# Attention weights transposed before they are scaled, with the scale applied to the values on leaving PSUM

## The chip, the core and the metric

The kernel runs on one core of one Trainium2 chip. The metric is the device time of one execution in microseconds (us). Three timed runs of the kernel before gave 3035.5, 3037.48 and 3040.55 us. The core has a matrix engine (TensorE, PE in the profile; its weight loads are PEld), VectorE (DVE), ScalarE (ACT) and GpSimd (POOL), and SyncE (SP), which here only issues DMAs. Each engine works through its own instructions in order.

## The reference

The input x has shape (4, 1024, 512). A graph attention layer comes first (part L0), then a transformer block conditioned on a vector (part L1). The change is within the attention of L1:

```python
qkv = x @ W_qkv                      # 16 heads of 64
attn = jnp.einsum('bqhd,bkhd->bhqk', q, k) * scale
attn = jax.nn.softmax(attn, axis=-1)
out = jnp.einsum('bhqk,bkhd->bqhd', attn, v).reshape(Bq, Tq, INNER)
return out @ W_out + b_out
```

Each of the 4 batch elements has 1024 rows, so each head has a 1024 x 1024 matrix of weights. Everything is in float32.

## The kernel before

The work has three stages: the graph attention (to about 400 us), the attention of L1 (to about 2235 us) and the MLP (to the end). Many of the large products are built of seven half-size products instead of eight, with sums made ahead by GpSimd and afterwards by VectorE.

**Slots.** The attention runs over 4 batch elements, 8 pairs of heads and 8 tiles of 128 query rows, that is 256 slots (variable `s`; `NS` = 256). A slot handles one tile `t` of one pair of heads; the two heads are `j` = 0 and 1. Two slots make a block `k` of 256 query rows (`QT` = 2 tiles). Within a slot:

- `scores` (L1151): eight matmuls, 64 rows deep, the two heads side by side, fill two PSUM tiles `psc` of 128 x 1024, one for each head. There are two such tiles in all, so the next slot's scores need this slot's exponentials done.
- `largest` (L1165): VectorE takes the negated row maximum of each head (`mx`, L1167).
- `weights` (L1170): ScalarE computes the exponential into an SBUF tile `w` (four buffers) and sums it along the row into `sm` (L1173).
- `scaled` (L1176): VectorE inverts the sum (L1178); head 0's weights are multiplied by it on ScalarE (L1180), head 1's on GpSimd (L1182).
- `turn` (L1184): VectorE transposes 32 x 32 pieces of `w` into the tile `wd` (L1191). `wd` holds one head's weights for both tiles of a block; its tag has three buffers, taken in turn. After the second tile, SP issues four DMAs of 256 KB (L1195) which move the four groups of 32 partitions of `wd` to their places in `wT`, so that keys lie along partitions. `wT` holds both heads of a block and has two buffers.
- `attend` (L1055): four slots after the block's first slot, 32 matmuls of values by weights, two heads side by side, sum up 128 x 256 in the PSUM tile `pav`; ScalarE copies it into `oT` (L1076).
- `out_step` (L1124): a part of the output projection, in the PSUM tile `pu`; VectorE adds it to the rows `xr` (L1148).

**Order.** The main loop (L1497) writes the order of a slot by hand. It first transposes head 0 of the slot before (`turn(..., 0)`), then does what is kept in `later` (copies and sums which empty PSUM after a projection step, on ScalarE and VectorE), then the scores, the two maxima, `early` (a part of the output projection that falls into the slot), the two exponentials, head 0's scaling, the transposition of head 1 of the slot before, and head 1's scaling. Last comes `emit`: the work that a planner (L1367 to L1447) has put into this slot, which is loads, attend, steps of the projections to q, k and v, parts of the output projection, and sums on GpSimd. The planner balances TensorE's work over the slots by the units given with each piece. Every engine gets its instructions in this order.

```python
            if before is not None:
                turn(*before[0], 0)
            while later:
                later.pop(0)()
```

The four lines above open a slot (L1498). VectorE's order in a slot is thus: transposition of head 0 (slot before), sums of `later`, maximum of head 0, maximum of head 1, an addition of `early`, inverse of sum 0, transposition of head 1 (slot before), inverse of sum 1, and the sums that `emit` brings.

Of the kernel before, what the change touches and what calls it, by code (L numbers as in the profile page):

```python
# [12 lines left out]
F32 = mybir.dt.float32  # L13
I32 = mybir.dt.int32
AF = mybir.ActivationFunctionType
ALU = mybir.AluOpType
# [3 lines left out]
P = 128  # L20
S = 1024
F = 512
FC = F // P
NT = S // P
# [8 lines left out]
H, D = 16, 64  # L33
# [8 lines left out]
def cond_block_kernel(  # L42
# [27 lines left out]
    nc = tc.nc  # L70
# [4 lines left out]
    def row(ap):  # L75

        return ap.unsqueeze(0)
# [46 lines left out]

    x1d = [tc.dram_tile([P, F], F32, name=f"x1d{i}") for i in range(NTA)]
    gated = tc.dram_tile([P, F], F32, name="gated")
    qrd = tc.dram_tile([B, F], F32, name="qrd")
    vrd = [tc.dram_tile([KV, F], F32, name=f"vrd{d}") for d in range(2)]
    x2d = [tc.dram_tile([P, F], F32, name=f"x2d{i}") for i in range(NTA)]
# [2 lines left out]
    with ExitStack() as gctx:  # L132
        KC0 = GH * 2 * NG // P
        HF = GH * NG
        gp = gctx.enter_context(tc.tile_pool(name="gp", bufs=1))
# [49 lines left out]
        with ExitStack() as sctx:  # L185
# [13 lines left out]
            rows = sp.tile([N_VEC, P], F32, name="rows")  # L199
# [8 lines left out]
            ws, gboB = [], sp.tile([KV, 2, F], F32, name="gboB")  # L208
# [365 lines left out]
        later = []  # L574
# [366 lines left out]
    with ExitStack() as actx:  # L941
        ap_ = actx.enter_context(tc.tile_pool(name="ap", bufs=1, reuse_waits="tile"))
        q1, q2 = (ps.tile([P, F], F32, name=n, tag=n) for n in ("q1", "q2"))
        two_banks = {"ma": q2, "mb": q1, "mc": q1, "md": q2}
        NP = 2 * NGRP
# [3 lines left out]
        QB = 256  # L949
        QT = QB // P  # L950
        NB = S // QB
        wout, gate = {}, {}
        vt, oT, xr, wn, wd, wT = {}, {}, {}, {}, {}, {}

        turns = []

# [98 lines left out]
        def attend(b, gp, k, a=0, z=KC):  # L1055

            if a == 0:
                pav[0] = ps.tile([P, F], F32, name="pav", tag="pav")[:, :QB]
            po = pav[0]
            g, p = divmod(gp, 2)  # L1060
            w = wT[b, gp, k]
            for m in range(a, z):
                for j in range(2):
                    nc.tensor.matmul(  # L1064
                        po[j * D : (j + 1) * D, :],
                        lhsT=vt[b, g][:, m, p * P + j * D : p * P + (j + 1) * D],
                        rhs=w[:, j, :, m, :],
                        start=(m == 0),
                        stop=(m == KC - 1),
                    )  # L1070
            if z < KC:
                return
            u, i = divmod(k, 2)
            if i == 0:
                oT[b, gp, u] = op_.tile([P, F], F32, name="oT", tag="oT", bufs=6)
            nc.scalar.copy(  # L1076
                oT[b, gp, u][:, i * QB : (i + 1) * QB].rearrange("p (t u q) -> p u t q", t=QT, u=4),
                po.rearrange("p (u t q) -> p u t q", t=QT, u=4),
            )

        def project(b, g, n):
# [69 lines left out]
        def scores(b, gp, t):  # L1151
            sc = [ps.tile([P, S], F32, name="psc", tag="sc", bufs=2) for _ in range(2)]
            for n in range(2):
                for j in range(2):
                    q = slice(j * D, (j + 1) * D)
                    nc.tensor.matmul(  # L1156
                        sc[j][:, n * F : (n + 1) * F],
                        lhsT=qT[b, gp][q, t * P : (t + 1) * P],
                        rhs=kT[b, gp][q, n * F : (n + 1) * F],
                        start=True,  # L1160
                        stop=True,
                    )
            return sc

        def largest(sc):  # L1165
            mx = ap_.tile([P, 1], F32, name="mx", tag="mx", bufs=4)
            nc.vector.tensor_reduce(mx, sc, axis=AX.X, op=ALU.max, negate=True)  # L1167
            return mx

        def weights(sc, mx):  # L1170
            w = ap_.tile([P, S], F32, name="w", tag="w", bufs=4)
            sm = ap_.tile([P, 1], F32, name="sm", tag="sm", bufs=4)
            nc.scalar.activation(w, sc, AF.Exp, bias=mx, accum_out=sm)  # L1173
            return w, sm

        def scaled(j, w, sm):  # L1176

            nc.vector.reciprocal(sm, sm)  # L1178
            if j == 0:
                nc.scalar.mul(w, w, sm)  # L1180
            else:
                nc.gpsimd.tensor_scalar(w, w, sm, None, ALU.mult)  # L1182

        def turn(b, gp, t, j):  # L1184

            k, at = divmod(t, QT)
            if at == 0:
                wd[j] = ap_.tile([P, 4 * KC, QT, U], F32, name="wd", tag="wd", bufs=3)
                if j == 0:
                    wT[b, gp, k] = ap_.tile([P, 2, 4, KC, QT * U], F32, name="wT", tag="wT", bufs=2)  # L1190
            nc.vector.transpose(wd[j][:, :, at, :], wn.pop((b, gp, t, j)).rearrange("p (m k) -> p m k", k=U))  # L1191
            if at == QT - 1:
                flat = wd[j].rearrange("p m t q -> p (m t q)")
                for u in range(4):
                    nc.sync.dma_start(  # L1195
                        wT[b, gp, k][:, j, u].rearrange("p m q -> p (m q)"), flat[U * u : U * (u + 1), :]
                    )
# [11 lines left out]
        def halves():  # L1209

            two = [ps.tile([P, S], F32, name="up", tag="sc", bufs=2) for _ in range(2)]
            return {n: two[k // 2][:, k % 2 * F : (k % 2 + 1) * F] for k, n in enumerate(("ma", "mb", "mc", "md"))}
# [5 lines left out]
        NS = B * NP * NT  # L1218
# [21 lines left out]
        for b in range(B):  # L1240
# [22 lines left out]
            for gp in range(NP):  # L1263
                g, p = divmod(gp, 2)
                at = s0 + gp * NT
# [12 lines left out]
                for k in range(NB):  # L1278
                    lo = at + QT * k + LAG
                    if gp == NP - 2:  # L1280

                        for h in range(2):
                            add(lo + h, lo + h, 1, 1, attend, b, gp, k, h * KC // 2, (h + 1) * KC // 2)
                        continue
                    add(lo, lo + (lo < NS - 8), 2, 1, attend, b, gp, k)
# [60 lines left out]
        for i in range(4):  # L1346
            at = NS - (10, 9, 6, 3)[i]
# [109 lines left out]
        def fill_of(s):  # L1457
            return [k for k in range(len(fill)) if where[k] == s]

        def emit(a, b):  # L1460


            for s in range(a, b):
                steps = {where[k] for k in chain}
                second = [k for k in outs if where[k] == s][1:]

                def place(k):
                    if k in inside:
                        at = 2.5 if s - 1 in steps else 0.5
                        if k in chain:  # L1470
                            return at
                        if k in second:
                            return 3.5
                        return min(at, 2) + 0.1 if s in steps else 2
                    return fill[k][3]

                for k in sorted(fill_of(s), key=lambda k: (place(k), k)):
                    if k not in done_early:
                        fill[k][4]()
                if s in steps and s - 1 not in steps and sum(fill[k][2] for k in fill_of(s)) >= 3:  # L1480
                    while later:
                        later.pop(0)()
# [3 lines left out]
        def early(s):  # L1486

            two = [k for k in outs if where[k] == s]
            sums = [k for k in fill_of(s) if fill[k][3] == -1]
            for k in two[: len(two) - 1] + sums:  # L1490
                fill[k][4]()
                done_early.add(k)

        row_sum(0, 2)
        emit(-3, 0)
        before = None
        for s in range(NS + 1):  # L1497
            if before is not None:  # L1498
                turn(*before[0], 0)
            while later:  # L1500
                later.pop(0)()
            if s < NS:
                b, r = divmod(s, NP * NT)
                gp, t = divmod(r, NT)
                sc = scores(b, gp, t)
                mx = [largest(sc[j]) for j in range(2)]
                early(s)
                ws = [weights(sc[j], mx[j]) for j in range(2)]
                now = ((b, gp, t), ws)
                scaled(0, *ws[0])  # L1510
            if before is not None:
                turn(*before[0], 1)
            before = None
            if s < NS:
                scaled(1, *ws[1])
                for j in range(2):
                    wn[(*now[0], j)] = ws[j][0]
                before = now
            if s < NS:
                emit(s, s + 1)  # L1520
        sc_banks = halves()
        late = []
        second = with_four(
# [25 lines left out]
    with ExitStack() as mctx:  # L1549
# [53 lines left out]
        for k in range(NB2):  # L1603
            b = k * VB // NT
# [3 lines left out]
            for p in range(2 if k == 0 else 0, 4):  # L1608
# [12 lines left out]
                elif p == 3:  # L1621
                    sums = []
                    for j in range(2):
                        o = [w2x[j][:, n] for n in range(3)]
                        q, r = w2s[j], w2s[2 + j]
# [97 lines left out]
```

## Time and profile before

| what | value |
|---|---|
| timed runs | 3035.5, 3037.48, 3040.55 us |
| profiled execution, its span | 3034.2 us |
| instructions | 41780 |
| DVE transposition of 128x1024 (L1191) | 512 x 1235 ns |
| DVE maximum of 128x1024 (L1167) | 512 x 1211 ns |
| ACT exponential (L1173) | 512 x 1115 ns |
| ACT scaling (L1180) | 256 x 1137 ns |
| POOL scaling (L1182) | 256 x 2846 ns |
| ACT copy of the values (L1076) | 128 x 359 ns (median) |
| DVE addition to the rows (L1148), 128x512 from PSUM | 210 x 683 ns |
| DMAs wT<-wd | 1024 of 256 KB |
| queue q1 (SP's DMAs) | 282256 packets, 415.03 MB, 53.8% of 16 engines' span |

The profile is of one execution; its span, from the first instruction to the last, is 3034.2 us, and the only other times at hand are the three timed runs, which lie 1.3 to 6.4 us above it. "Busy" is the time in which an engine works on data; issuing DMAs and waiting aren't busy. A row of the timeline gives start, length, engine, line and operation, what it writes and reads, and how often; brackets at its end give the idle time of the engine before it and who ended it. A row with x2 or x8 stands for so many instructions in a row. The chain of waits is followed back from the last instruction, at each step to what released it; "SPq" is the issuing of a DMA, "DMA" the time from its issue to its landing.

### The profile page before, as it was taken

The numbers are of one execution on the slowest core, as the hardware profiler recorded it, in microseconds if no ns is written. First come the engines' busy times: TensorE is split into PE (matmuls) and PEld (weight loads), VectorE is DVE, ScalarE is ACT, GpSimd is POOL, SyncE is SP. The second block draws the span as 40 slices with busy tenths as digits, with TensorE's granted clock in tenths as the row PEclk, the third lists the DMA queues.
The fourth block names the chain that finished last, engine by engine and source line by source line (L and its number), as shares of the span: only waits on it lengthen the run. The fifth ranks groups of instructions, "written<-read, shape, count | busy, mean of one in ns | idle before, by whom it ended". The sixth has DMA issues, their size and how long they took to land.

```text
span 3034.2 us, 41780 instructions
## 1 busy us (share of the span) xinstructions
PE 2999.3 (99%) x15317; PEld 1980.2 (65%) x15317; DVE 1999.6 (66%) x2836; ACT 1432.0 (47%) x2368; POOL 1339.4 (44%) x922
## 2 busy tenths in 40 slices
PE   9999999999999999999999999999999999999999
PEld 6666655555555555555555555555568888888888
DVE  3888867777878877878787878877863222222322
ACT  3344456555755565755555755556641221112211
POOL 1444456555656655656655656655721110111010
PEclk9999999999999999999999999999999999999999
DMA  6433357777868777768777868766871010101110
GB/s 201 140 118 121 117 129 180 162 171 179 192 157 210 181 168 179 192 155 211 187 159 180 191 159 205 189 162 164 203 196 63 14 49 28 49 21 35 35 42 15
DMA packets 282695, 417.90 MB, mean 138 GB/s; under 512 B 28968, under 2 KB 101092, under 8 KB 282492
## 3 DMA queue, kind: packets, MB, share of 16 engines
q1 hardware_dynamic: 282256, 415.03, 53.8%
q8 instruction: 123, 2.02, 0.3%
q14 instruction: 80, 0.66, 0.1%
q10 hardware_dynamic: 236, 0.20, 0.0%
HBM read 120.93 MB, written 25.76 MB: 48 GB/s over the span
## 4 chain that ended last, share of the span: by engine, by line
PE 83%; DVE 7%; ACT 3%; POOL 3%; issue 2%; DMA 2%; SPq 1%; POOLq 0%; DVEq 0%; ACTq 0%
PE q L533 19%; PE psc L1156 15%; PE pav L1064 13%; PE pu L1139 6%; PE mbd L533 5%; PE mbu L533 5%; PE mad L533 4%; PE mau L533 3%; PE mcd L533 2%; PE mdd L533 2%; PE mdu L533 2%; PE mcu L533 2%; DVE mx L1167 1%; ACT w L1173 1%; POOL t L742 1%
## 5 line engine op out<-in xcount | busy, mean ns | idle before, releaser
L1182 POOL TENSOR_SCALAR w<-w,sm 128x1024 f32<-128x1024 f32 x256 | 728.6, 2846 | 701.5 <-DVE sm L1178 686.4
L1173 ACT ACTIVATE w<-psc,mx 128x1024 f32<-128x1024 f32 x512 | 570.7, 1115 | 642.6 <-DVE mx L1167 641.6
L1191 DVE STREAM_TRANSPOSE wd<-w 128x1024 f32<-128x1024 f32 x512 | 632.2, 1235 | 109.3 <-ACT w L1180 96.0
L1167 DVE TENSOR_REDUCE mx<-psc 128x1 f32<-128x1024 f32 x512 | 599.2, 1211 | 80.2 <-PE psc L1156 77.0
L1156 PE MATMUL psc<-kT,qT 64*128 64x512 f32 x2048 | 526.9, 615 | 3.1 <-ACT kT L1024 1.4
L1064 PE MATMUL pav<-wT,v 128*64 128x256 f32 x4096 | 482.1, 383 | 1.2 <-DMA wT<-wd 0.6
L1064 PEld LDWEIGHTS pav<-wT,v 128*64 128x64 f32 x4096 | 296.1, 137 | 224.0 <-issue 86.0
L1156 PEld LDWEIGHTS psc<-kT,qT 64*128 64x128 f32 x2048 | 201.6, 186 | 220.5 <-issue 151.2
L1180 ACT ACTIVATE w<-w,sm 128x1024 f32<-128x1024 f32 x256 | 291.0, 1137 | 0.0
L512 POOL TENSOR_TENSOR tx<-hT 128x512 f32<-128x512 f32 x8 | 10.3, 1288 | 596.5 <-ACT hT L448 596.5
L1148 DVE TENSOR_TENSOR xr<-pu,xr 128x512 f32<-128x512 f32 x210 | 143.5, 683 | 78.9 <-PE pu L1139 78.7
L533 PE MATMUL q<-hT,wqk 128*128 128x512 f32 (+1 forms) x396 | 181.2, 581 | 1.0 <-DVE q L547 1.0
L555 ACT COPY mbu<-mau 128x512 f32<-128x512 f32 x30 | 17.1, 570 | 276.5 <-PE mau L533 276.5
L719 PE MATMUL pa<-kp,sfT 128*128 128x320 f32 x512 | 143.5, 433 | 1.4 <-ACT sfT L694 1.4
L533 PEld LDWEIGHTS q<-hT,wqk 128*128 128x128 f32 x396 | 74.7, 190 | 80.9 <-issue 78.2
L533 PE MATMUL q<-tx,ex 128*128 128x512 f32 (+1 forms) x264 | 123.5, 591 | 1.8 <-POOL tx L618 1.3
L719 PEld LDWEIGHTS pa<-kp,sfT 128*128 128x128 f32 x512 | 94.8, 190 | 38.2 <-ACT sfT L694 1.9
L679 PE MATMUL pf<-wx,xT 128*128 128x512 f32 x256 | 116.0, 596 | 0.0
L533 PE MATMUL mad<-w,hs 128*128 128x256 f32 x512 | 113.1, 379 | 0.0
L533 PEld LDWEIGHTS mad<-w,hs 128*128 128x128 f32 x512 | 97.3, 190 | 13.2
L1139 PE MATMUL pu<-wout,oT 128*128 128x256 f32 x360 | 98.4, 396 | 4.2 <-DVE xr L1148 3.7
L1139 PEld LDWEIGHTS pu<-wout,oT 128*128 128x128 f32 x360 | 62.6, 189 | 59.3 <-issue 31.6
(309 smaller groups left out, 4590.7 us busy)
## 6 DMA issues: line engine op xcount, KB each, us to landing
wT<-wd SPq DMA_DIRECT2D x1024, 256.0 KB
wqk<-in_w_qkv SPq DMA_DIRECT2D x64, 256.0 KB
xT<-in_xt SPq DMA_DIRECT2D x32, 256.0 KB
xs<-in_x SPq DMA_DIRECT2D x32, 256.0 KB
x1d<-xs SPq DMA_DIRECT2D x32, 256.0 KB
xl<-x1d SPq DMA_DIRECT2D x32, 256.0 KB
wv<-in_w_qkv SPq DMA_DIRECT2D x32, 256.0 KB
xr<-x1d SPq DMA_DIRECT2D x32, 256.0 KB
```

What stands on the lines that cost most here:

```text
L533: nc.tensor.matmul(t[:, q * width : (q + 1) * width], lhsT=lhs(which, q, k), rhs=rhs(which, q, k), start=(fresh and q == 0 and k == 0), st ...
L679: nc.tensor.matmul(pfs[i], lhsT=xT[i][:, c, :], rhs=wx[:, c, :], start=False, stop=(c == FC - 1), skip_group_check=True,)
L719: nc.tensor.matmul(pas[i][:, n, :HF], lhsT=sfT2[i][:, c, :], rhs=kp[:, b, c, n * HF : (n + 1) * HF], start=False, stop=(c == FC - 1), skip ...
L1064: nc.tensor.matmul(po[j * D : (j + 1) * D, :], lhsT=vt[b, g][:, m, p * P + j * D : p * P + (j + 1) * D], rhs=w[:, j, :, m, :], start=(m == 0),
L1139: nc.tensor.matmul(pu[0][:, q * HB : (q + 1) * HB], lhsT=a[:, q * P : (q + 1) * P], rhs=r, start=(bool(fresh) and q == 0), stop=True, skip ...
L1148: nc.vector.tensor_tensor(o, pu[0].rearrange("p (r f) -> p r f", r=2), o, ALU.add)
L1156: nc.tensor.matmul(sc[j][:, n * F : (n + 1) * F], lhsT=qT[b, gp][q, t * P : (t + 1) * P], rhs=kT[b, gp][q, n * F : (n + 1) * F], start=Tru ...
L1167: nc.vector.tensor_reduce(mx, sc, axis=AX.X, op=ALU.max, negate=True)
L1173: nc.scalar.activation(w, sc, AF.Exp, bias=mx, accum_out=sm)
L1180: nc.scalar.mul(w, w, sm)
L1182: nc.gpsimd.tensor_scalar(w, w, sm, None, ALU.mult)
L1191: nc.vector.transpose(wd[j][:, :, at, :], wn.pop((b, gp, t, j)).rearrange("p (m k) -> p m k", k=U))
```

## The change

The row sums are no longer divided out of the weights. Each head's weights are transposed in their own slot, right after the exponential, unscaled. `w` has two buffers in place of four. The sums of a block (two heads, two tiles) are gathered in one tile of 128 x 4, inverted once by VectorE, written to a small DRAM tile with one DMA issued by ScalarE one slot after the block, and read back one slot later with two DMAs, also issued by ScalarE, each of which spreads 256 values over the 64 partitions of a head (`rB`). When `attend` is done, VectorE multiplies the PSUM tile by `rB` into `oT`, where ScalarE copied it before. What the planner puts into the slots is unchanged, and so are the buffers of `wd` and `wT`.

```diff
+    scd = [tc.dram_tile([4, P], F32, name=f"scd{i}") for i in range(4)]
...
+        esum, scales, rB, spot = {}, {}, {}, [0]
...
-            nc.scalar.copy(
+            nc.vector.tensor_tensor(
                 oT[b, gp, u][:, i * QB : (i + 1) * QB].rearrange("p (t u q) -> p u t q", t=QT, u=4),
                 po.rearrange("p (u t q) -> p u t q", t=QT, u=4),
+                rB.pop((b, gp, k)).rearrange("p (t u q) -> p u t q", t=QT, u=4),
+                ALU.mult,
             )
...
-        def weights(sc, mx):
-            w = ap_.tile([P, S], F32, name="w", tag="w", bufs=4)
-            sm = ap_.tile([P, 1], F32, name="sm", tag="sm", bufs=4)
-            nc.scalar.activation(w, sc, AF.Exp, bias=mx, accum_out=sm)
-            return w, sm
-
-        def scaled(j, w, sm):
-
+        def weights(b, gp, t, j, sc, mx):
+            k, at = divmod(t, QT)
+            w = ap_.tile([P, S], F32, name="w", tag="w", bufs=2)
+            if (b, gp, k) not in esum:
+                esum[b, gp, k] = ap_.tile([P, 2 * QT], F32, name="sm", tag="sm", bufs=2)
+            c = j * QT + at
+            nc.scalar.activation(w, sc, AF.Exp, bias=mx, accum_out=esum[b, gp, k][:, c : c + 1])
+            wn[b, gp, t, j] = w
+
+        def scales_out(b, gp, k):
+
+            sm = esum.pop((b, gp, k))
             nc.vector.reciprocal(sm, sm)
-            if j == 0:
-                nc.scalar.mul(w, w, sm)
-            else:
-                nc.gpsimd.tensor_scalar(w, w, sm, None, ALU.mult)
+            spot[0] += 1
+            scales[b, gp, k] = scd[spot[0] % len(scd)]
+            return lambda: nc.scalar.dma_start(scales[b, gp, k].rearrange("c p -> p c"), sm)
+
+        def scales_in(b, gp, k):
+
+            rows = scales.pop((b, gp, k))
+            rB[b, gp, k] = ap_.tile([P, QB], F32, name="rB", tag="rB", bufs=2)
+            for j in range(2):
+                nc.scalar.dma_start(
+                    rB[b, gp, k][j * D : (j + 1) * D, :],
+                    row(rows[j * QT : (j + 1) * QT, :].rearrange("t q -> (t q)")).broadcast_to([D, QB]),
+                )
...
-        before = None
-        for s in range(NS + 1):
-            if before is not None:
-                turn(*before[0], 0)
+        coming = []
+        for s in range(NS):
             while later:
                 later.pop(0)()
-            if s < NS:
-                b, r = divmod(s, NP * NT)
-                gp, t = divmod(r, NT)
-                sc = scores(b, gp, t)
-                mx = [largest(sc[j]) for j in range(2)]
-                early(s)
-                ws = [weights(sc[j], mx[j]) for j in range(2)]
-                now = ((b, gp, t), ws)
-                scaled(0, *ws[0])
-            if before is not None:
-                turn(*before[0], 1)
-            before = None
-            if s < NS:
-                scaled(1, *ws[1])
-                for j in range(2):
-                    wn[(*now[0], j)] = ws[j][0]
-                before = now
-            if s < NS:
-                emit(s, s + 1)
+            b, r = divmod(s, NP * NT)
+            gp, t = divmod(r, NT)
+            sc = scores(b, gp, t)
+            mx = [largest(sc[j]) for j in range(2)]
+            early(s)
+            for j in range(2):
+                weights(b, gp, t, j, sc[j], mx[j])
+            for j in range(2):
+                turn(b, gp, t, j)
+            while coming and coming[0][0] <= s:
+                coming.pop(0)[1]()
+            if t % QT == QT - 1:
+                key = b, gp, t // QT
+                coming.append((s + 1, scales_out(*key)))
+                coming.append((s + 2, lambda key=key: scales_in(*key)))
+            emit(s, s + 1)
+        while later:
+            later.pop(0)()
+        for _, f in coming:
+            f()
```

## The prediction

> **What bounds the kernel now.** I read the page first, then the busy time by stretches, then TensorE's own waits, then the timeline of one pair of attention slots.
>
> ```profile
> PE 2999.3 (99%) x15317; PEld 1980.2 (65%) x15317; DVE 1999.6 (66%) x2836; ACT 1432.0 (47%) x2368; POOL 1339.4 (44%) x922
> ```
>
> TensorE is busy 99% of the span. The Trainium skill ("Perfetto Trace Analysis", Identifying the Most-Contended Engine) speaks against trusting this number: matmul busy time is a bad metric because matmuls are pipelined, and the weight loads' share (here 65%) is the better one, which would leave room for a large gain. So I looked at the pace and at the waits.
>
> ```profile
> 425.00:860.00 435.00, 430.33 (x2311) 244.67 (x2311) 346.27 (x442) 269.81 (x421) 267.10 (x170) 1.00 0.75 179
> 860.00:1325.00 465.00, 462.70 (x2519) 264.02 (x2516) 374.17 (x486) 277.28 (x434) 284.00 (x185) 1.00 0.75 182
> 1325.00:1790.00 465.00, 461.55 (x2510) 262.83 (x2510) 375.49 (x488) 278.43 (x434) 281.53 (x182) 1.00 0.74 178
> 1790.00:2235.00 445.00, 442.48 (x2366) 251.60 (x2364) 363.20 (x477) 263.16 (x410) 268.70 (x179) 1.00 0.75 181
> ```
>
> ```profile
> PE pu L1139 <- DVE xr L1148: 3.7, 6, 1.0
> ```
>
> The columns of the stretches (first fence) are PE, weight loads, DVE, ACT, POOL, clock, share of the DMA engines and GB/s. The change touches only these 1810 us of attention. TensorE is busy for 1797.06 of them, and its longest sum of waits in the whole run (second fence) is 3.7 us. The 32 value matmuls of a block take 3.60 us nearly every time they stand in the chain of waits. **So no more than about 13 us can be won**, whatever work ScalarE and GpSimd lose. The question is what new wait reaches TensorE.
>
> ```profile
> 601.35 1.99 PE L1156 MATMUL psc<-kT,qT 64*128 64x512 f32 x8
> 602.95 1.22 DVE L1191 STREAM_TRANSPOSE wd<-w 128x1024 f32<-128x1024 f32 x1
> 604.10 2.32 DVE L1167 TENSOR_REDUCE mx<-psc 128x1 f32<-128x1024 f32 x2
> 604.24 8.76 SPq L1195 DMA_DIRECT2D wT<-wd  x8
> 605.32 1.11 ACT L1173 ACTIVATE w<-psc,mx 128x1024 f32<-128x1024 f32 x1 [3.92 <-DVE mx L1167]
> 606.64 1.23 DVE L1191 STREAM_TRANSPOSE wd<-w 128x1024 f32<-128x1024 f32 x1
> 607.62 1.14 ACT L1180 ACTIVATE w<-w,sm 128x1024 f32<-128x1024 f32 x1
> 608.78 1.25 DVE L1191 STREAM_TRANSPOSE wd<-w 128x1024 f32<-128x1024 f32 x1 [0.87 <-ACT w L1180]
> 610.80 2.36 DVE L1167 TENSOR_REDUCE mx<-psc 128x1 f32<-128x1024 f32 x2 [0.77 <-PE psc L1156]
> 613.51 1.25 DVE L1191 STREAM_TRANSPOSE wd<-w 128x1024 f32<-128x1024 f32 x1
> ```
>
> Call the two heads of a slot 0 and 1, and their transpositions T0 and T1. A block is two slots, 2k and 2k+1. At 602.95 is T0 of slot 2k-1, already one slot late; it completes head 0 of block k-1, and 0.07 us after its end SP begins to issue that head's four DMAs (then the other head's four, x8 in all). 606.64 is T1 of slot 2k-1. 608.78 is T0 of slot 2k and 613.51 T1 of slot 2k.
>
> **The wait that decides.** The tile wd has three buffers, used in turn by (block k-1, head 0), (k-1, 1), (k, 0), (k, 1). So T1 of slot 2k, the first write of (k, 1), takes the buffer of (k-1, 0), and has to wait until the four DMAs issued at 604.24 have read it. In the trace it is T0 and T1 of even slots alone that wait on DMA semaphores. How long these DMAs take, from the chain of waits of a window:
>
> ```profile
> 1833.89 1.25 DVE wd L1191
> ...
> 1835.16 0.55 SPq L1195
> ...
> 1835.75 0.60 SPq L1195
> ...
> 1836.40 5.76 DMA wT<-wd
> ```
>
> From the end of the transposition (1835.14) to the landing of the third DMA (1842.16) are 7.0 us, and the fourth comes later. Taking for all 128 head-0 groups the last of the landing records, the time from T0's end is 7.86 us on the mean (5th to 95th percentile 7.4 to 8.5). Now T1 of slot 2k starts 613.51 - 604.17 = 9.3 us after T0's end; over all blocks 10.4 us (median; 8.7 to 12.3). The landing is covered.
>
> **Part 1: the transposition moves into its own slot.** The order on DVE was T0 (late), two maxima, T1 (late); it becomes two maxima, T0, T1. T1 follows T0 at once: the second exponential ends 1.2 us after the first, and a transposition lasts 1.24. So the distance from T0's end in slot 2k-1 to T1 in slot 2k becomes one slot. The scores in this timeline start at 601.35, 608.78, 615.33, 620.85 and 627.60, so slots are 5.5 to 7.4 us; their mean is 7.1. That is **less than 7.86: T1 waits in nearly every block, by some 0.8 us**, and behind it on DVE queue the additions of the output product (xr, L1148), the evacuations for the next projection step, and the maxima of the next slot, for which ScalarE's exponentials and then TensorE's scores wait.
>
> A wait is harmless while DVE has slack, so I add up the closed ring of one block: landing 7.86; start after it 0.06; T1 1.24; DVE's other work up to the next maxima; the two maxima 2.34; first exponential ready 0.15 later; T0 of slot 2k+1 1.24. The fixed terms give 12.89. The other work, summed for each block from the DVE rows between these instructions (without the old reciprocals, with 0.42 for the new product below), is 1.25 on the mean: **ring 14.14 us**. The blocks, from scores to scores of every second slot, are 14.21 us on the mean, but from 11.3 to 17.5: 55 of 127 are shorter than their own ring, by 1.39 us each (76 us), and 72 are longer, by 80 us. Blocks can lend to each other only what lateness TensorE doesn't feel: second exponential ready 3.6 us after the maxima start, after 2.0 us of scores, in slots of 5.5 to 7.4 us leaves 0 to 1.8 us; I take 1.0. Carrying lateness from block to block (never below 0, what is above 1.0 us counted as TensorE standing) gives **54 us**. With headroom 1.5 and landing 7.4 it is 27 us or a little more; with 0.5 and landing 8.26, 88 us.
>
> **Part 2: scaling removed.** ScalarE loses 256 x 1.14 us and 128 copies of 0.36 us, GpSimd 256 x 2.85 us, DVE 512 reciprocals of 0.12 to 0.16 us. All of it lies beside TensorE. What it frees: T0 waits for ScalarE's scaling in 119 slots (up to 0.9 us; one such wait is the bracket at 608.78). This wait goes, and the landing is late next. From the 13 us I credit 5; bounds 0 and 13.
>
> **Part 3: product on leaving PSUM.** 128 DVE products of 128x256 from PSUM. Not in the trace at that size; below 0.68 (the L1148 addition, 512 wide), and near 0.36 (the ScalarE copy it replaces); 0.42 taken, in the ring above. DVE's sum per slot stays: -0.28 reciprocals, +0.21 product, +0.07 new reciprocal. If it were 0.68, 0.26 us more in each ring, some 16 us; the range has it.
>
> **Part 4: sums through DRAM on ScalarE's queue.** For each block one write of 128x4 elements and two broadcast reads to 64 partitions. ScalarE issues three DMAs more per block at 0.3 to 1.0 us (SP's 321 ns for qrd, its 0.5 to 1.3 us here); it is idle for 4 of 7 us, so this hides. The read waits for the write's landing with later copies and the next exponentials queued behind it; the write is issued one slot, about 7 us, earlier. The nearest rows: qrd, written at 34.6 and read from 36.6 (2.0 us), and vrd, written at 38.5 and read from 42.8 (4.3 us). No wait then. The write's effect on other DMAs: below, nothing (2 KB); above, every element costs as much as a mean packet of the queue, 0.538 x 16 x 3034 us / 282256 = 93 ns, which is 3.0 us of each DMA engine per block. Only the last 1 us of a head-0 group lies beside it. Between 0 and 0.8 us of landing I take 0.1: from 54 us at 7.86 to 80 us at 8.26 the slope is 65 us per us, so +6. The Trainium skill ("DMA: Bandwidth & Descriptors", Rules for kernel authors) warns against exactly this write: a strided last dimension becomes one descriptor per element, 512 here. By that rule I would take the upper bound, and +50 us instead of +6.
>
> After the loop the last write and its read stand back to back on ScalarE: 3 us once.
>
> **Sum.** 54 - 5 + 6 + 3 = 58 us on the profiled execution, whose span is 3034.2; the three timed runs lie 1.3 to 6.4 us above it. From their median 3037.5 I predict **3095 us**.
>
> **Rivals.**
> - Gain. The landing isn't binding (it would have to be under the slot, some 7.0 us, or the headroom nearly 2 us), T0's waits for ScalarE go, and TensorE gets back up to 10 of 13 us: 3027. For: DVE is busy 5.7 of 7.1 us only. Against: 7.4 us is the 5th percentile of landings.
> - No difference. The same with the stalls cancelling: 3031 to 3044 (0.2% is 6 us, about what a measurement can tell from no change).
> - ScalarE blocked. If the element-wise write lands later than 7.1 us after its issue, the read stands at the head of ScalarE's queue. Idle ScalarE time covers some 2.5 us, so from about 9.6 us on each further us costs 128 us; a landing of 12 us gives 3037 + 58 + 300 = 3400.
>
> **Chances.** Ring as forecast, 3050 to 3180: 66%. Slower by less, 3044 to 3050: 4%. Within 0.2%: 10%. Faster: 8%. Above 3180 by ScalarE's queue or crowded DMAs: 12%. The range 3032 to 3180 leaves out two tenths (faster, and above). Faster 0.08, same 0.10, slower 0.82.
>
> **What would show it.** Right: in the changed profile DVE's transposition waits for the DMA wT<-wd about once a block, some 100 to 200 us in sum; TensorE's idle time in attention grows from 13 us to about 70, behind maxima, exponentials and xr additions; blocks shorter than 13 us disappear. Wrong: that wait is small (landing under 7 us, or lateness absorbed), or ScalarE waits for the written sums.

## The result, and the profile after

| | median, us | lowest to highest | ratio to before, 95% interval |
|---|---|---|---|
| before (four runs) | 3039.02 | 3035.5 to 3046.95 | |
| changed (four runs) | 3228.53 | 3218.56 to 3250.59 | 1.0628 [1.0587, 1.0669] |

The change makes the kernel 190 us slower; 58 us were forecast, and the time lies 49 us above the range. The profiled execution is the longest of the four (3250.59 us, span 3248.8).

The page of the changed kernel first: the engines, the two DMA queues that the kernel's own transfers use (packets, MB, share of 16 engines), and the chain that ended last. The single line behind it is the chain of the kernel before.

```profile
PE 3096.0 (95%) x15317; PEld 2004.2 (62%) x15317; DVE 2009.3 (62%) x2580; ACT 1128.5 (35%) x1984; POOL 613.7 (19%) x666
...
q1 hardware_dynamic: 282256, 415.03, 52.6%
q10 hardware_dynamic: 88300, 17.27, 3.2%
...
PE 59%; DMA 18%; DVE 8%; SPq 6%; issue 3%; ACT 3%; POOL 2%; ACTq 1%; DVEq 0%; POOLq 0%
```

```profile
PE 83%; DVE 7%; ACT 3%; POOL 3%; issue 2%; DMA 2%; SPq 1%; POOLq 0%; DVEq 0%; ACTq 0%
```

ScalarE lost 304 us of work (1432 to 1128; 338 were counted) and GpSimd 725 (1339 to 614; 729 were counted), and TensorE went from 99% busy to 95%. In the chain, DMAs hold 18% and SP's issuing 6%; before the change they held 2% and 1%. Queue q10, which had 236 packets in the kernel before, now carries ScalarE's three small DMAs of each block. It takes only 3.2% of the DMA engines' time. What the rows below show is not a lack of throughput but late landings.

The same four stretches of attention that the prediction showed, with the same columns:

```profile
425.00:860.00 435.00, 406.90 (x2090) 223.91 (x2088) 317.98 (x346) 176.61 (x294) 73.79 (x94) 0.98 0.77 172
860.00:1325.00 465.00, 445.81 (x2294) 246.55 (x2290) 339.69 (x380) 180.96 (x304) 94.06 (x112) 0.97 0.77 171
1325.00:1790.00 465.00, 441.76 (x2297) 246.19 (x2298) 345.54 (x388) 179.79 (x301) 94.09 (x112) 0.97 0.78 172
1790.00:2235.00 445.00, 408.37 (x2080) 222.01 (x2078) 319.42 (x358) 170.81 (x286) 80.29 (x94) 0.97 0.76 170
```

TensorE stands for 19 to 37 us in each stretch, where it stood for 2 to 5 us, and something else is new: the granted clock is 0.97 or 0.98, where it was 1.00. Attention now ends at about 2440 us in place of 2235. The waits between 430 and 2420 us, TensorE's, VectorE's and SP's:

```profile
PE pu L1143 <- DVE xr L1152: 49.4, 32, 6.3
PE psc L1160 <- ACT w L1180: 37.7, 33, 3.1
...
PE pav L1066 <- DMA wT<-wd: 11.9, 9, 2.3
```

```profile
DVE wd L1208 <- DMA wT<-wd: 203.5, 100, 8.2
...
DVE wd L1208 <- DMA scd<-sm: 48.8, 17, 6.6
```

```profile
...
SPq L1212 <- DMA wT<-wd: 85.1, 40, 5.1
SPq L1212 <- DMA wqk<-in_w_qkv: 41.7, 35, 3.8
```

The second fence is the forecast wait: the transposition waits for the DMAs wT<-wd, 100 times, 203.5 us. But it also waits for scd<-sm, the small write of the sums, with which it shares no data, and SP, whose waits in the attention of the kernel before name no landing at all, now waits for landings 158 times, 217 us in sum (third fence, the two longest groups of them). What happens in one block, in rows of the timeline:

```profile
1011.06 0.37 ACTq L1189 DMA_DIRECT2D scd<-sm  x1
...
1016.11 2.36 DVE L1208 STREAM_TRANSPOSE wd<-w 128x1024 f32<-128x1024 f32 x2
...
1016.70 0.19 ACT L1180 ACTIVATION_READ_ACCUMULATOR w<-psc,mx 128x1 f32 x1
...
1019.71 1.10 ACTq L1196 DMA_DIRECT2D rB<-scd  x2
...
1020.21 9.01 SPq L1212 DMA_DIRECT2D wT<-wd  x8
...
1028.42 1.25 DVE L1208 STREAM_TRANSPOSE wd<-w 128x1024 f32<-128x1024 f32 x1 [3.98 <-DMA wT<-wd]
```

The write of the sums is issued at 1011.06. By the landing records it lands at 1019.69, 8.6 us later, though it is 2 KB. Three things wait for that moment. ScalarE has been done since 1016.89, and its next instruction, the read of the sums, goes out at 1019.71. One of the DMAs wT<-wd, issued at 1010.72, is recorded as landed at 1020.13. And SP issues the next group not right behind T0, whose end is at about 1017.3, but at 1020.21, right behind that landing, since its DMA takes over the same completion semaphore (the one that tells of a landing); so T1 of the next slot finds its buffer still unread at 1024.4 and waits 3.98 us.

### The profile page after: what moved, and what is told of

The parts are those of the page before. It is cut to its first block, busy times and chain, and to the rows that moved or that the text cites. A ratio compares the mean times of both kernels' runs of the same rounds, so it can differ in the third digit from the quotient of the medians.

```text
span 3248.8 us, 41642 instructions
## 1 busy us (share of the span) xinstructions
PE 3096.0 (95%) x15317; PEld 2004.2 (62%) x15317; DVE 2009.3 (62%) x2580; ACT 1128.5 (35%) x1984; POOL 613.7 (19%) x666
## 4 chain that ended last, share of the span: by engine, by line
PE 59%; DMA 18%; DVE 8%; SPq 6%; issue 3%; ACT 3%; POOL 2%; ACTq 1%; DVEq 0%; POOLq 0%
PE q L534 12%; PE psc L1160 9%; PE pav L1066 7%; DMA wT<-wd 7%; PE mbd L534 5%; SPq L1212 5%; PE mbu L534 5%; DMA scd<-sm 4%; PE mad L534 3%; PE pu L1143 3%; PE mau L534 3%; DVE mx L1171 2%; PE mcd L534 2%; PE mdd L534 2%; PE mdu L534 2%
## 5 line engine op out<-in xcount | busy, mean ns | idle before, releaser
L1208 DVE STREAM_TRANSPOSE wd<-w 128x1024 f32<-128x1024 f32 x512 | 620.9, 1233 | 322.7 <-DMA wT<-wd 205.9
L1160 PE MATMUL psc<-kT,qT 64*128 64x512 f32 x2048 | 575.7, 634 | 41.4 <-ACT w L1180 37.7
L1066 PE MATMUL pav<-wT,v 128*64 128x256 f32 x4096 | 497.2, 390 | 12.1 <-DMA wT<-wd 11.9
L534 PE MATMUL q<-hT,wqk 128*128 128x512 f32 (+1 forms) x396 | 189.6, 604 | 13.2 <-DVE q L548 13.2
L505 POOL TENSOR_TENSOR ex<-wqk 128x256 f32<-128x256 f32 x33 | 24.0, 728 | 687.3 <-issue 281.7
L1180 ACT ACTIVATION_READ_ACCUMULATOR w<-psc,mx 128x1 f32 x512 | 99.3, 194 | 0.0
```

The costliest lines, as they stand in the source:

```text
L505: e.tensor_tensor(o[0], a21, a22, ALU.add)
L534: nc.tensor.matmul(t[:, q * width : (q + 1) * width], lhsT=lhs(which, q, k), rhs=rhs(which, q, k), start=(fresh and q == 0 and k == 0), st ...
L1066: nc.tensor.matmul(po[j * D : (j + 1) * D, :], lhsT=vt[b, g][:, m, p * P + j * D : p * P + (j + 1) * D], rhs=w[:, j, :, m, :], start=(m == 0),
L1160: nc.tensor.matmul(sc[j][:, n * F : (n + 1) * F], lhsT=qT[b, gp][q, t * P : (t + 1) * P], rhs=kT[b, gp][q, n * F : (n + 1) * F], start=Tru ...
L1180: nc.scalar.activation(w, sc, AF.Exp, bias=mx, accum_out=esum[b, gp, k][:, c : c + 1])
```

## The experiments

Two theories stood at the start. **Ring**: the third buffer of wd costs 54 us as forecast, and the rest is the same ring with later landings. **Trip**: the way of the sums through DRAM costs more than the ring, by itself (the expectations call this the DRAM theory). They can be switched off one by one: a fourth buffer of wd (a tile of the first stage, `gates`, was moved to another pool to make room) takes the ring away; a constant in place of the inverse sums takes the trip away.

### Ring and trip apart: four kernels

**e1_wd4**: changed kernel, `tag="wd", bufs=4`.

> The changed kernel with four wd buffers in place of three (room for it: the tile gates moves to the pool of the first stage). T1 of an even slot then takes the buffer of (k-2, head 1), which has long been read. Ring theory (T1's wait for its wd buffer is nearly all of the +190 us): 3035 to 3070. DRAM theory (the element-wise write of the sums lands after 8.7 us, holds ScalarE's queue and the DMA lanes; the ring is only the 54 us that were worked out): 3130 to 3190. Under both, DVE's waits for the landing of wT<-wd fall from 206 us to under 30.

**e2_nodram**: changed kernel, no trip:

```diff
-                coming.append((s + 1, scales_out(*key)))
-                coming.append((s + 2, lambda key=key: scales_in(*key)))
+                scales_out(*key)
...
```

> The changed kernel without the three DMAs of a block: the sums are still inverted, but the product on leaving PSUM takes a constant tile (1/1024), so the weights are not normalised. Order, buffers and DVE work stay. Ring theory: 3150 to 3230, little changed. DRAM theory: the landing returns to 7.9 us and the ring costs what was forecast, 3070 to 3110.

**e3_nodram_wd4**: both.

> Both at once: four wd buffers and no DMAs of the sums (constant tile in the product, weights not normalised). Both theories: all of the loss is gone, 3025 to 3045, and TensorE's idle time in attention is back at some 13 us. If it stays above 3060, a third cause is in the new order itself (output additions and evacuations behind T1).

**e4_before_dram**: the kernel before with the three DMAs per block added, and nothing else of the change (`gates` is moved here too).

> The kernel before with the three DMAs of a block added on ScalarE's queue at the same distance of one slot (they carry a constant and nobody uses what they bring), the old order and the old scaling kept. Ring theory: 3037 to 3050, since the wd buffers have 10.4 us there. DRAM theory: 3080 to 3160, ScalarE's queue held by the read that waits for the write.

Measured, against 3038.06 us of the kernel before (3039.02 for the changed kernel):

| | three wd buffers | four wd buffers |
|---|---|---|
| with the trip | 3228.53 (changed kernel) | e1: 3185.81, ratio 1.049 [1.0472, 1.0507] |
| without it | e2: 3076.45, ratio 1.0124 [1.0109, 1.0139] | e3: 3016.8, ratio 0.9927 [0.9912, 0.9942] |

e4: 3199.79, ratio 1.0528 [1.0512, 1.0544]. e1 and e2 lie where the trip theory had them; e3 lies below its range and e4 above.

The ring costs 60 us without the trip (e2 less e3) and 43 us with it. **The trip costs 152 us with three buffers, 169 us with four, and 162 us in the kernel before**. It needs no other part of the change. The ring is slack in the kernel before, where transpositions wait for wT<-wd 6 times, 3.9 us in sum. With the trip added, in e4, they wait for it there too:

```profile
DVE wd L1206 <- DMA wT<-wd: 220.3, 98, 4.5
```

e2 shows the ring by itself, as VectorE's longest wait:

```profile
DVE wd L1210 <- DMA wT<-wd: 199.3, 122, 4.0
```

122 waits, once a block; 199 us of VectorE's waiting cost the kernel 60 us, the rest is slack. In e1 this wait is gone, and TensorE's first line shows what is left with the trip:

```profile
PE pav L1066 <- DMA wT<-wd: 50.1, 33, 5.3
PE psc L1160 <- ACT w L1180: 25.2, 19, 3.9
```

and SP's own waits for landings have grown:

```profile
SPq L1212 <- DMA wT<-wd: 153.5, 80, 5.2
```

### Which part of the trip: write, read, or the queue

**e5_wd4_write** writes the sums and does not read them; **e6_wd4_read** reads rows that were written once. **e7_wd4_early** is e1 with the write one slot earlier, between T0 and T1, so that the read finds it landed. Three explanations are told apart here: the queue (ScalarE's queue is held by the read that waits), the semaphores (late landings hold up the DMAs that come after), and crowding (512 small packets slow the others).

> Four wd buffers, the write of the sums at its old place, no reads (a constant tile in the product; weights not normalised). With no reads the kernel takes 3017, with write and reads 3186. Queue theory (the loss is ScalarE's queue, held by the read that waits for the write): 3017 to 3030. Semaphore theory (the DMAs take turns with eight completion semaphores, each DMA waits until the one eight before it has landed, so SP's issues of wT<-wd wait for the slow write): 3070 to 3150, and SP's waits on DMAs stay at some 100 to 200 us. Crowding theory (512 small packets slow the wT<-wd packets themselves): also 3070 to 3150, but SP doesn't wait on DMAs.

> Four wd buffers, the two reads of a block at their old place, but no writes in the loop: they read DRAM rows that were written once ahead of it with a constant (weights not normalised). Queue theory: 3017 to 3030, since nothing holds the reads. Semaphore theory: 3017 to 3045, two more DMAs in the turn, which land in some 4 us. Above 3060 both are wrong.

> Four wd buffers, everything computed, but the write is issued in its own slot, between T0 and T1, and the reads two slots later as before: 14 us lie between them, so no read waits for its write. Queue theory: 3017 to 3050. Semaphore theory: 3090 to 3170, since the write still lands after some 9 us and holds its semaphore.

e5: 3114.61, ratio 1.0256 [1.0232, 1.028]. e6: 3025.09, ratio 0.9955 [0.9941, 0.997]. e7: 3177.39, ratio 1.0455 [1.0431, 1.0478]. From e3's 3016.8 the write alone costs 98 us and the reads alone 8 us. So the write is the larger part of the 169 us, although in e5 no read waits for it. The other 63 us are there only when write and reads are there together. e7 does not tell what they are. It takes most of the reads' waiting off ScalarE's queue (55 us over all reads, 295 in e1) and is only 8 us quicker, but other waits grow: SP's for landings from 302 to 503 us, and a new one, of VectorE's product for the reads:

```profile
DVE oT L1078 <- DMA rB<-scd: 207.7, 91, 4.7
```

Landing records say how the write costs so much. In e5 it lands 8.8 us after its issue (median), although the last of its 512 packets starts 4.1 us after it and each takes 9 ns. A DMA wT<-wd issued within 1 us behind it lands 8.7 us after its own issue, 0.16 to 0.34 us after the write (10th to 75th percentile of some 80 cases); those that overlap no write take 4.8 us. So **other DMAs' landings wait for the slow write's**. The Trainium skill ("DMA: Bandwidth & Descriptors", Queues, rings and completion order) has the rule for this: a DMA's semaphore increment is a strongly ordered write, which lands only after every earlier write of that DMA engine, across its queues. The records agree with it, and 0.16 to 0.34 us is what it looks like. SP is caught too: SP's and ScalarE's DMAs take eight completion semaphores in turn, and each waits for the landing of the one that held its semaphore before. In the changed kernel 17% of the DMAs are issued within 0.3 us behind such a landing, in the kernel before 1.6%. In e5 SP waits 112 us for landings, as the semaphore theory had it.

### What makes the write slow

**e8_wd4_runs** is e7 with the inverse sums first transposed by VectorE (128x32), so that the write is 128 runs of 128 B; the reads become 256 runs of 256 B each:

```diff
+            smT = ap_.tile([P, U], F32, name="smT", tag="smT", bufs=2)
+            nc.vector.transpose(smT, sm)
...
-            return lambda: nc.scalar.dma_start(scales[b, gp, k].rearrange("c p -> p c"), sm)
+            return lambda: nc.scalar.dma_start(scales[b, gp, k], smT)
```

> As e7_wd4_early, but the inverted sums are first transposed on DVE (128x32, some 0.1 us), so that the write is 128 runs of 128 bytes in place of 512 elements of 4, and each read 256 runs of 256 bytes. Semaphore theory: the write lands in 2 to 4 us like the other writes to DRAM, holds nothing, 3017 to 3045, faster than the kernel before or the same. Crowding theory by number of packets: between, 3050 to 3110. Queue theory: as e7_wd4_early.

e8: 3088.65, ratio 1.0163 [1.0146, 1.018], 89 us below e7. The write lands after 3.65 us, and the DMAs wT<-wd issued within 1 us behind it after 5.4 us. The time is above what the semaphore theory allowed and in the range of crowding by the number of packets. Four kernels with the write alone, as e5, say whether the number of elements or their addresses count. **e11** puts the 512 elements 2048 B apart in DRAM, **e15** 512 B, **e14** 64 B (its diff is below); **e12** writes 128 runs of 16 B, one after the other.

```diff
-    scd = [tc.dram_tile([4, P], F32, name=f"scd{i}") for i in range(4)]
+    scd = [tc.dram_tile([4, P, 16], F32, name=f"scd{i}") for i in range(4)]
...
-            return lambda: nc.scalar.dma_start(scales[b, gp, k].rearrange("c p -> p c"), sm)
+            return lambda: nc.scalar.dma_start(scales[b, gp, k][:, :, 0].rearrange("c p -> p c"), sm)
```

> e5_wd4_write (four buffers of wd, the write alone, nothing reads it, the product is with a constant 1/1024) with the 512 elements of 4 bytes 2048 B apart in DRAM in place of lying in 4 rows of 512 B. If the slow landing (8.7 us) is that of 512 separate elements, it stays at 8 us or more and the time near 3115. If it comes from neighbouring elements meeting in the same line of DRAM, the landing falls below 5 us and the time to 3020 to 3050.

> e5_wd4_write with the sums kept as they lie in SBUF: 128 runs of 16 B, one for each partition, in place of 512 of 4 B; nothing reads them, the product is with a constant. If the number of elements sets the landing, it is near 3.65 us (128 runs of 128 B in e8_wd4_runs) and the time 3020 to 3040. If the meeting of small pieces in one line of DRAM does (four of these runs lie in 64 B), it stays above 6 us and the time above 3060.

> e11_wd4_write_apart (the write alone, 512 elements of 4 B) with the elements 64 B apart in DRAM in place of 2048 B. If it is elements within the same 64 B that slow each other, the landing is below 5 us as at 2048 B (4.74) and the time 3015 to 3022. If a larger piece of DRAM (a page, a bank) does, the landing is 6 us or more and the time 3040 to 3115.

> The same 512 B apart. If e14_wd4_write_apart64 is already quick, this is the same, 3015 to 3022. If it is slow, this shows whether 512 B are enough (below 5 us) or not (6 us or more).

| write alone, four wd buffers | lands after (median) | time, us | ratio to before |
|---|---|---|---|
| e5: 512 x 4 B, side by side | 8.8 us | 3114.61 | 1.0256 [1.0232, 1.028] |
| e14: 512 x 4 B, 64 B apart | 4.8 us | 3019.29 | 0.9936 [0.9921, 0.9951] |
| e15: 512 x 4 B, 512 B apart | 4.9 us | 3018.65 | 0.9941 [0.9927, 0.9956] |
| e11: 512 x 4 B, 2048 B apart | 4.7 us | 3017.81 | 0.9923 [0.9907, 0.9938] |
| e12: 128 x 16 B, side by side | 4.2 us | 3017.11 | 0.9921 [0.9908, 0.9934] |
| e3: no write | | 3016.8 | 0.9927 [0.9912, 0.9942] |

It is not the number of elements: the same 512 elements, 64 B apart, cost 2.5 us instead of 98. **Pieces of 4 B side by side are what is slow**; four pieces of 16 B in 64 B are not, so sharing 64 B does not by itself make a write slow. Distances between 4 and 64 B, and pieces of 8 B, were not tried. The chain that ended last, of e5 and then of e14:

```profile
PE 69%; DMA 14%; SPq 5%; DVE 5%; issue 3%; POOL 2%; ACT 1%; POOLq 0%; ACTq 0%; DVEq 0%
```

```profile
PE 85%; DVE 6%; POOL 3%; DMA 2%; issue 2%; SPq 1%; ACT 1%; POOLq 0%; ACTq 0%; DVEq 0%
```

The two kernels issue the same instructions and move the same packets (q10 has 67820 in both, of 9 ns each); only addresses in DRAM differ, and DMA's share of the chain falls from 14% to 2%. What happens inside the memory the runs don't show.

### What is left when the write is quick

e8 still lies 72 us above e3. Its ScalarE rows:

```profile
1005.51 0.33 ACTq L1194 DMA_DIRECT2D scd<-smT  x1
1005.94 2.70 ACTq L1202 DMA_DIRECT2D rB<-scd  x2
1008.68 0.59 ACT L1050 COPY v<-q 128x512 f32<-128x512 f32 x1 [3.66 <-DVE v L552]
```

Write and reads of two blocks fall into one slot, and an evacuation waits behind them. **e9_wd4_runs_late** puts the write back one slot later, **e10_wd3_runs_late** is the same with three buffers, and **e16_wd4_runs_apart** is e9 with reads that don't depend on the write.

> e8_wd4_runs with the write of the inverse sums (128 runs of 128 B) put back to the place it has in the changed kernel: one slot after the block, so that write and reads of two neighbouring blocks stand in different slots on ScalarE's queue. Everything is computed. If what e8_wd4_runs still lost (3088.65 against 3016.8 of e3_nodram_wd4) is the 3.7 us in which three DMA issues in one slot hold ScalarE and its evacuations, then at most about 2.7 us are held in one slot, ScalarE's idle time covers most of that, and the time is 3020 to 3040, faster than the kernel before or level with it. If it is the landing of the longer reads (5.8 us) or the write's effect on other DMAs, the time stays at 3070 to 3095.

> The same with three buffers of wd, as in the changed kernel: only the shape of the write is mended. The ring of the third buffer alone cost 60 us without the trip (e2_nodram against e3_nodram_wd4). If ring and trip add, this lies 50 to 65 us above e9_wd4_runs_late, 3075 to 3100, slower than the kernel before. If instead the ring were worth little once the write is quick, it would lie within 15 us of e9_wd4_runs_late.

> e9_wd4_runs_late with write and reads of the same shape and place, but not dependent on each other: the sums are written to tiles that nobody reads, and the reads fetch a constant (1/1024) from tiles that were written once. If the wait of the read for the write on ScalarE's queue is the larger part of the 24 us, this lies at 3022 to 3028 (the 8 us that reads alone cost, and little else). If traffic and issues are the larger part, it stays at 3033 to 3042.

e9: 3040.58, ratio 1.0007 [0.9997, 1.0017], **no different from the kernel before, while everything is computed**. e9 differs from e1, and e10 from the changed kernel, only in the shape of write and reads and in VectorE's small transposition: that is worth 145 and 142 us, most of the trip, the read's wait for the late write included. e10: 3086.21, ratio 1.0145 [1.0131, 1.016]: 46 us above e9, a little less than the 50 to 65 expected, so ring and trip roughly add. VectorE's first wait in e10 is the ring again:

```profile
DVE wd L1214 <- DMA wT<-wd: 170.2, 110, 3.9
```

e16: 3031.21, ratio 0.9974 [0.9963, 0.9984], between the two ranges that were expected of it, so neither cause is the larger part by itself. If the pieces add, of e9's 24 us above e3 9 are the read's wait for the write (e9 less e16), 8 are reads (e6), and 6 are left for the transposition of the sums, the write and the shorter runs of the reads together.

**e13_wd4_runs_1k** was to take away the short runs of the reads, with four DMAs of 4 runs of 128 B for the write:

> e9_wd4_runs_late with the inverse sums written as 16 runs of 128 B by four DMAs of ScalarE (one for each 32 queries), so that they lie in DRAM as in the changed kernel and each read is 64 runs of 1 KB again in place of 256 runs of 256 B. Everything is computed. If the 24 us that e9_wd4_runs_late still lies above e3_nodram_wd4 come from the reads' 256 B runs and longer issue (0.62 us each in place of 0.50), the time falls to 3020 to 3030, faster than the kernel before (3039). If they come from ScalarE being held by the trip (the read that waits for the write, and the issues), it stays at 3035 to 3055, since there are three more issues of 0.33 us per block.

e13: 3146.47, ratio 1.0358 [1.0343, 1.0373], far beyond both. The reads do land sooner (2.65 us in place of 3.52), but:

```profile
1004.94 4.20 ACTq L1197 DMA_DIRECT2D scd<-smT  x4
...
1009.25 1.11 ACT L1183 ACTIVATE w<-psc,mx 128x1024 f32<-128x1024 f32 x1 [4.41 <-DMA scd<-smT]
```

Four issues of 0.25 us each take ScalarE 4.20 us, with the next exponential behind them: each goes out 0.02 to 0.03 us after the landing of the DMA that held its completion semaphore before. Since e13 changes two things, it says nothing of the reads' shape; that stays open.

**e17_wd4_runs_sp** hands the write to SP, one slot earlier.

> e9_wd4_runs_late with the write of the inverse sums (128 runs of 128 B) issued by SP instead of ScalarE, right behind the block's last four DMAs wT<-wd and so one slot earlier; the reads keep their place on ScalarE's queue. Everything is computed. e16_wd4_runs_apart priced the read's wait for the write at about 9 us. If that is what this takes away, the time is 3028 to 3034, faster than the kernel before (3039). If the write on SP's queue holds up the next block's DMAs, or if it lands too late behind them, it is 3038 or more.

e17: 3059.79, ratio 1.0076 [1.0063, 1.0089], worse than e9. SP's queue has the block's transfers in front of it:

```profile
999.76 4.06 SPq L1218 DMA_DIRECT2D wT<-wd  x3
...
1003.92 0.54 SPq L1194 DMA_DIRECT2D scd<-smT  x1
```

The write goes out 7.7 us (median) after its data are ready, and the reads of 19 blocks still hold ScalarE for more than 1 us (some 55 us over all blocks, against 22 in e9). The earlier place was lost again in the queue.

### The credit for the removed scaling

e3 is 21 us faster than the kernel before, where the prediction saw at most 13. **e18_before_unscaled** takes Part 2 by itself into the kernel before:

```diff
-            nc.vector.reciprocal(sm, sm)
-            if j == 0:
-                nc.scalar.mul(w, w, sm)
-            else:
-                nc.gpsimd.tensor_scalar(w, w, sm, None, ALU.mult)
+            return
```

> The kernel before with Part 2 alone: the weights are not scaled and no inverse is taken (the values are multiplied by a constant 1/1024 in ScalarE's copy instead); the late transposition, w's four buffers and wd's three stay. The prediction credited this with 5 us and at most 13, which gives 3026 to 3034. e3_nodram_wd4, 22 us below the kernel before, says that more is to be had: if all of it comes from the scaling, this is 3015 to 3020; if it comes from the transposition in its own slot with a fourth buffer, this stays at 3030 or above.

e18: 3026.55, ratio 0.9962 [0.9948, 0.9975], 11.6 us less. So the removed scaling gives 11.6 us, and what else e3 has, the transposition in its own slot with a fourth buffer and the product on VectorE, another 10. In TensorE's busy time that is:

```profile
PE 2994.5 (99%) x15317; PEld 1965.0 (65%) x15317; DVE 1941.8 (64%) x2324; ACT 1166.9 (39%) x2112; POOL 613.6 (20%) x666
```

and in e3:

```profile
PE 2984.2 (99%) x15317; PEld 1963.5 (65%) x15317; DVE 2002.6 (66%) x2581; ACT 1124.9 (37%) x1984; POOL 614.6 (20%) x666
```

The number of matmuls is the same, their busy time falls from 2999.3 to 2994.5 and 2984.2: so part of what the page calls busy can be won. What it consists of the runs don't show.

## Why the prediction was wrong

- **What bounds the kernel**: right that TensorE does, and that only a new wait could matter. The bound of 13 us for the gain was too tight: without the trip and the ring (e3) the rest of the change gives 21 us. It was taken from idle time alone, and busy time also held 15 us that went.
- **Part 1, the ring**: right in mechanism and size. Forecast 54 us; 60 us in e2 against e3 (43 us beside the trip). The landing after T0's end was taken as 7.86 us and is 7.98 in e2; in the changed kernel the trip makes it 9.2. That the size is so near is in part luck: the headroom of 1.0 us was chosen out of 0 to 1.8, and the prediction itself had 27 us with 1.5 and 88 with 0.5, each with another landing.
- **Part 2**: 5 us credited, 0 to 13 allowed; 11.6 measured (e18).
- **Part 3**: 0.42 us taken for the product, 0.39 measured (128 products in e3); ScalarE's copy was the right neighbour.
- **Part 4 is the step that failed.** "No wait then" rested on rows of qrd and vrd, 2.0 and 4.3 us, which write rows of 2 KB and not elements of 4 B; the write of the sums lands after 8.7 us, later than the slot of about 7 us that it was given. The "+6" for its effect on other DMAs looked at throughput, at most 93 ns for each element (its packets take 9 ns); the cost is in landings that wait for this one, in SP's turns of the semaphores, and in ScalarE's queue. All of Part 4 was 9 us with the end; it is 152. The upper bound, 0.8 us of landing and +50 us, was too low as well, since a late landing reaches every DMA in flight and not the last 1 us of one group. The rule of the Trainium skill ("DMA: Bandwidth & Descriptors", Rules for kernel authors) that the prediction weighed would have given that bound. It points at the right instruction, but the number of descriptors is not the reason: as many separate elements 64 B apart cost 2.5 us (e14).
- **The rival "ScalarE blocked"** had its condition right (a landing above 7.1 us) and by its own price, nothing below 9.6 us, it would have given no loss at 8.7 us. In the profile 61 reads wait more than 1 us, some 155 us in sum. What that alone costs is not shown: with four buffers it is at most the 63 us that write and reads cost only together, and e7 does not settle it, since e7 brings waits of its own.
- **What would show it**: the transposition's wait of 100 to 200 us came (203.5), but its cost, 43 to 60 us, is less than a third of the whole. TensorE's idle time in attention went to some 125 us, not 70. Blocks shorter than 13 us did not disappear: 25 of 127 still are, where 46 were. "ScalarE waits for the written sums", given as a sign of error, was there.
- **The chances**: a case above 3180 by crowded DMAs or ScalarE's queue had 12%, and it is what came, by the crowding of landings rather than of data.

Half-clock stretches of TensorE, told below, are part of the 152 us and were in no step.

## What to carry to other kernels

Price a small DMA by when it lands and by which other DMAs land behind it, not by its bytes: look for a row with the same size of pieces and the same distance between them, and, where there is none, keep a wide range or write pieces of at least 16 B, or elements 64 B apart, which were quick here. A DMA issued by a compute engine puts three waits into that engine's queue, for its data, for its turn of a semaphore and for its issue; count them per slot against the engine's idle time there. A two-by-two of "with and without" each suspected cost (here ring and trip) settles with four kernels what a single profile, in which one delay shows up as another's wait, does not.

## What the runs showed of the hardware that was not expected

**Neighbouring 4-byte writes.** 512 elements of 4 B in four rows of 512 B land 8.7 to 8.8 us after the issue; 64 B apart, 4.8 us; as 128 runs of 16 B, 4.2 us.

**The matmul clock after a stall.** In the changed kernel the granted clock falls to 0.5 in 24 stretches within attention, of 3.41, 6.83 or 10.24 us, 130 us in all. All 24 belong to a stall of TensorE of 1.5 to 10.0 us: they begin within it or at most 1.7 us behind its end. Of the 26 stalls of 1.9 us or more, three (2.6, 2.6 and 3.4 us) had no such stretch behind them. Stretches around one of them (PE, weight loads, DVE, ACT, POOL, clock, DMA share, GB/s), and TensorE's rows:

```profile
1030.90:1034.03 3.13, 0.03 (x1) 0.00 (x0) 2.89 (x5) 1.25 (x3) 2.80 (x4) 1.00 0.64 98
1035.22:1042.05 6.83, 6.83 (x22) 2.96 (x24) 4.42 (x7) 1.28 (x2) 0.00 (x0) 0.50 0.74 211
```

```profile
1034.04 4.89 PE L1160 MATMUL psc<-kT,qT 64*128 64x512 f32 x8 [3.11 <-ACT w L1180]
1038.86 5.22 PE L1066 MATMUL pav<-wT,v 128*64 128x256 f32 x32
```

After 3.11 us of standing, the eight score matmuls take 4.89 us in place of 1.99, and the 32 value matmuls 5.22 in place of 3.6. Half clock in attention: 130 us in the changed kernel, 68 in e1, 82 in e7, 24 in e5, 20 in e2, none in the kernel before, e3 and e18. In the changed kernel TensorE is busy in 118 of the 130 us; if half of that is lost, it is an estimated 59 us of the kernel's time, behind stalls of 75 us in sum. The Trainium skill ("TensorE: Matmul & The Clock Gate", Why this matters for your kernels) asks for no gaps of more than about 3 us, and gives a window of 3413 ns in Part 1. Here 17 of the 24 stalls were shorter than 3 us, and the stretches are multiples of that window.
